# Ten units of the products with B on GpSimd instead of nine, in a four-layer kernel of selective scans

## The chip, the cores and the metric

The kernel runs on one core of one Trainium2 chip. The metric is the device time of one execution in microseconds (us). Engine names follow the profile: PE is TensorE, DVE is VectorE, ACT is ScalarE, POOL is GpSimd, SP is SyncE, which only issues DMAs here.

## The reference

Eight images of 48 x 48 positions with 96 channels pass through four layers, each `x = x + layer(group_norm(x))`. Layers 0 and 3 (l0, l3) are selective scans over four directions of the image (rows and columns, both ways), layer 1 is an upsampling with a two-layer network between, layer 2 (l2) is again four selective scans, but over single rows and columns of 48 positions. The scan at the heart of three of the four layers is

```python
def step(h, inp):
    u, dl, Bv, Cv = inp
    dA = jnp.exp(dl[..., None] * A)
    h = h * dA + (dl * u)[..., None] * Bv[:, :, None, :]
    y = jnp.einsum('bkdn,bkn->bkd', h, Cv)
    return (h, y)
```

for 4 directions, 192 channels and 16 states: per position a product of `dl * u` with B, the recurrence, and a product with C that is summed over the states.

## The kernel before, in words

Each of the three scan layers runs `scans` (L188), which walks through blocks. A block is one image, one direction and 10 of its 48 rows (480 positions, or 8 rows and 384 positions for the last of five): 8 x 4 x 5 = 160 blocks a layer. In l0 and l3 the scan runs on across the rows (a block has 4 columns more for the carried state, so tiles are 481, 484 or 962 wide); in l2 it starts anew at each row.

A block is worked on in four turns, called q0 to q3 here, and each turn in two slots, so slots 0 to 7. A slot holds three units: 3 tiles of 128 partitions (32 channels by 4 states). A turn therefore has six units, and its scans take them in three pairs. The order is written out by hand in the loop at L386 to L418. In turn t:

- DVE: `scan(t, 0)`, `make_dbu(at + 2)`, `scan(t, 1)`, `make_dbu(at + 3)`, `scan(t, 2)`. The scan (L300) is one instruction for two units. `make_dbu` (L268) multiplies `dl * u` by B for the two slots of the next turn, so slots 6 and 7 are made in q2, slots 4 and 5 in q1, slots 2 and 3 in q0.
- POOL: `make_hc(t-1, 1)` (L306, the product with C of a whole slot, in place), then its own part of `make_dbu` for the next turn's two slots, then `begin` (a small copy or zero, L277 or L280), then `make_hc(t, 0)`.
- ACT: `make_da` (L292, the exponential for two units, into one of two PSUM buffers), `copy_b` (L249), and side steps.
- PE: `reduce` (L326, L328), which sums the products with C over the states into `ps_y`, behind the `make_hc` of the turn before, and side steps.

Which units of a slot POOL makes is the table that the change edits: `ON_POOL_SS` for l0 and l3, `ON_POOL_L2` for l2 (L43, L44). The value is the number of the slot's units, its last ones, that POOL makes; DVE makes the others. DVE reads B from a PSUM copy (`ps_b`, one buffer) that ACT writes in `copy_b`; POOL reads B from SBUF. Where a slot is all POOL's, no copy is made:

```python
if on_pool.get(slot) == 3:
    return
if slot == NG // 2 and t - 1 in bps:
    bps[t] = bps[t - 1]
    return
```

so slot 4 takes slot 3's copy over where there was one (in l2).

`aside` (L370) runs, once a slot, the steps that prepare the blocks to come (`stage1`), the end of the outputs (`done`), and a side generator (the convolution of the next image and the normalization of the last one in l0 and l3). Some of these change ACT's function and need a table load before and another before the next exponential. In l0 and l3 it is the softplus (L678) in slot 6, that is in q3, and in part of the blocks the SiLU of the next image's convolution (L538, L540). In l2 it is the SiLU of u (L799) in slot 6, in q3; the softplus (L827) in slot 0, in q0; and the SiLU of the gate, zb (L842), in slot 2, in q1. In l2, PE runs `project` (L864) in slot 2 and the two convolutions (L792) in slots 3 and 4; `done` multiplies `ps_y` by zb on DVE (L855), once in q0 and once in q2; L870 or L872 add the projection in slot 3.

DMAs are all issued on SP: `store_dd` (L446) writes `dl` and `dl * u` to DRAM, `load_dd` (L221) and `load_bc` (L233) bring them back, broadcast over partitions, into three buffers and seven buffers.

Of the kernel before, what the change touches and what calls it, by code (L numbers as in the profile page):

```python
# [39 lines left out]
FAR = 1e30  # L40
CH = 96

ON_POOL_SS = {2: 1, 3: 3, 5: 1, 6: 1, 7: 3}  # L43
ON_POOL_L2 = {3: 2, 5: 3, 6: 1, 7: 3}  # L44


DIRS_SS = [(False, False), (True, False), (False, True), (True, True)]
# [50 lines left out]
def vss_stack_kernel(ctx: ExitStack, tc: tile.TileContext, i: dict, out: bass.AP):  # L98
# [372 lines left out]
    def ss2d(l, xin, xout, b0=0):  # L471
# [41 lines left out]
        def conv(b, blks, behind=lambda step: step()):  # L513
            if blks[0] == BLKS[0]:
                us[b] = big.tile([DH, 2, L], F32, tag="big", name="u")
                zs[b] = zdr.tile([DH, 2, L], F32, tag="z", name="zd")
            for r0, nr in blks:
                n = nr * SEG
                for half in range(2):
                    pu = side_psum()  # L520
                    for slot in range(7):
                        for tap in ((0,), (1, 2), (3,), (4, 5), (6,), (7, 8), ())[slot]:
                            dy, dx = tap // 3, tap % 3
                            at = (2 * tap + half) * DH
                            nc.tensor.matmul(pu[:, :n], lhsT=flat[:, at:at + P],  # L525
                                             rhs=xpad[:, r0 + dy:r0 + dy + nr, dx:dx + W],
                                             start=(tap == 0), stop=(tap == 8))
                        if slot == 6:
                            got = {}

                            def gate():
                                got["z"] = ps("s1", 1)
                                nc.tensor.matmul(got["z"][:DH, :n], lhsT=w[f"{l}_in"][:, (2 + half) * DH:(3 + half) * DH],
                                                 rhs=xpad[:C, 1 + r0:1 + r0 + nr, 1:1 + W], start=True, stop=True)
                            behind(gate)
                        yield
                    s = slice(r0 * W, r0 * W + n)
                    nc.scalar.activation(us[b][:, half, s], pu[:DH, :n], AF.Silu, bias=w[f"{l}_cb"][:, half:half + 1])  # L538
                    z = zp.tile([DH, BMAX], F32, tag="z", name="z")
                    nc.scalar.activation(z[:, :n], got["z"][:DH, :n], AF.Silu)  # L540
                    yield
                    nc.sync.dma_start(zs[b][:, half, s], z[:, :n])
# [164 lines left out]
        for _ in conv(0, BLKS[:1]):  # L707
            pass
        scans(dirs, (0, 1, 3, 2), False, ON_POOL_SS, a, pools, ps, stage1, opening, done, side, tail, conv(0, BLKS[1:3]))
        for _ in post(nb - 1, BLKS[:1]):  # L710
# [4 lines left out]
    def lines(xin, xout):  # L715
# [172 lines left out]
        dirs = DIRS_L2  # L888
        scans(dirs, range(NK), True, ON_POOL_L2, a, pools, ps, stage1, opening, done, side, tail)
        stack.close()  # L890
# [288 lines left out]
```

## Time and profile before

| | us |
|---|---|
| median of 3 runs (18397.58 to 18422.25) | 18410.51 |
| the profiled execution | 18410.93 |
| its span in the trace | 18409.2 |
| scans of l0 in the trace, from 107 to 5561 | 5454 |
| scans of l2, from 6978 to 12808 | 5830 |
| scans of l3, from 12924 to 18381 | 5457 |

The 1.7 us between the execution and its span lie outside the first and last instruction. What is left between the three stretches is layer 1 (5561 to 6978) and short preparations. In the profile, a group's row gives the line, engine, operation, written and read tiles, shape and count, then the busy time, the mean duration in ns, and the idle time before it with what ended it.

### The profile page before, as it was taken

Reading aid. Unit: us, or ns where it says so; the run is one execution under the profiler, and the core shown is the slowest. Engines: PE = TensorE matmul, PEld = TensorE weight load, DVE = VectorE, ACT = ScalarE, POOL = GpSimd, SP = SyncE. Lnnn points to the kernel's source line nnn. Section 1 sums busy time; section 2 is a strip of 40 time slices with the busy share of each in tenths; the row PEclk is TensorE's granted clock in tenths of the full one; section 3 lists DMA queues with packets and bytes.
Section 4 is the critical chain, followed back from the end, with each engine's and each line's share of the span. In section 5 each row is a group of like instructions: output and inputs, shape, how many; then the busy total and the mean of one; then the engine's idle time right before and its main releaser. Section 6 shows DMA issues by size and latency. Waiting matters only on the chain.

```text
span 18409.2 us, 167554 instructions
## 1 busy us (share of the span) xinstructions
PE 14747.1 (80%) x53500; PEld 4297.8 (23%) x53500; DVE 16140.7 (88%) x10329; ACT 13666.8 (74%) x20348; POOL 15136.4 (82%) x7999
## 2 busy tenths in 40 slices
PE   7777777777777897888988988988777777777777
PEld 1211211211214562222222222222121221221221
DVE  7999999999992228999999999997899999999998
ACT  6877887887772227888788888886788778778776
POOL 7999999999990007888888888887899999999998
PEclk7877877777767787888888888888778778777776
DMA  4544545544443324444444444443454455455454
GB/s 143 175 171 171 172 172 172 174 174 167 172 168 52 50 43 148 158 150 152 156 149 156 150 155 156 148 155 125 164 178 171 169 173 173 170 175 173 166 174 144
DMA packets 768448, 2836.47 MB, mean 154 GB/s; under 512 B 235724, under 2 KB 298668, under 8 KB 640926
## 3 DMA queue, kind: packets, MB, share of 16 engines
q1 hardware_dynamic: 767558, 2825.75, 45.4%
q8 instruction: 418, 6.85, 0.2%
q14 instruction: 472, 3.87, 0.1%
HBM read 2377.32 MB, written 448.17 MB: 153 GB/s over the span
## 4 chain that ended last, share of the span: by engine, by line
POOL 27%; PE 20%; DVE 16%; issue 14%; ACT 14%; DMA 8%; SPq 1%; POOLq 0%; ACTq 0%; DVEq 0%
POOL dbu L306 18%; DVE dbu L300 10%; POOL dbu L268 6%; PE ps_s L792 5%; ACT ps_da L292 5%; DVE dbu L268 4%; DMA dd<-dds 3%; POOL dds L460 3%; PE ps_y L326 3%; ACT L292 2%; DMA dd<-dd 2%; PE ps_h L998 2%; PE ps_y L1011 2%; PE ps_s L864 1%; ACT L827 1%
## 5 line engine op out<-in xcount | busy, mean ns | idle before, releaser
L300 DVE TENSOR_TENSOR_SCAN dbu<-ps_da,dbu 128x968 f32<-128x968 f32 (+3 forms) x5760 | 11820.3, 2075 | 559.7 <-ACT ps_da L292 447.5
L306 POOL TENSOR_TENSOR dbu<-dbu,bc 128x1440 f32<-128x1440 f32 (+1 forms) x3840 | 10061.9, 2633 | 1615.3 <-DVE dbu L300 1540.9
L292 ACT ACTIVATE ps_da<-dd,w_l_a 128x484 f32<-128x484 f32 (+3 forms) x11520 | 7433.6, 649 | 2878.2 <-DVE dbu L300 2651.5
L326 PE MATMUL ps_y<-dbu,w_red 128*32 128x480 f32 (+1 forms) x23040 | 4838.4, 735 | 1955.6 <-POOL dbu L306 1935.4
L328 PE MATMUL ps_y<-dbu,w_red 128*32 128x480 f32 (+1 forms) x7680 | 4797.9, 735 | 0.0
L268 DVE TENSOR_TENSOR dbu<-dd,ps_b 128x962 f32<-128x962 f32 (+5 forms) x2880 | 3833.4, 1331 | 264.9 <-ACT ps_b L249 150.6
L268 POOL TENSOR_TENSOR dbu<-dd,bc 128x481 f32<-128x481 f32 (+5 forms) x2240 | 3910.5, 1760 | 22.6 <-DMA dd<-dd 19.5
L326 PEld LDWEIGHTS ps_y<-dbu,w_red 128*32 128x32 f32 x23040 | 748.5, 124 | 5975.6 <-POOL dbu L306 4242.9
L792 PE MATMUL ps_s<-xpad,w_l_cw 128*128 128x480 f32 (+1 forms) x2560 | 1758.5, 839 | 0.0
L249 ACT COPY ps_b<-bc 128x482 f32<-128x482 f32 (+3 forms) x2720 | 1450.5, 533 | 233.4 <-DVE dbu L268 191.4
L525 PE MATMUL ps_side<-xpad,w_l_cw 128*128 128x480 f32 (+1 forms) x2880 | 1526.5, 657 | 18.9 <-ACT u L538 14.2
L292 ACT ACT_TABLE_LOAD x986 | 1265.0, 1283 | 17.6
L734 POOL MEMSET xpad<- 128x2760 f32 x2 | 4.7, 2404 | 1333.9 <-DVE x L978 1333.9
L322 PE MATMUL ps_y<-ysum,w_ident 96*96 96x480 f32 (+1 forms) x960 | 762.9, 885 | 315.9 <-ACT ysum L701 315.3
L650 PE MATMUL ps_s<-bcl,dtw 6*96 6x480 f32 (+1 forms) x1280 | 871.7, 770 | 103.7 <-ACT dds L654 93.2
L660 PE MATMUL ps_s<-u,w_l_xp 96*38 96x480 f32 (+1 forms) x1280 | 832.3, 781 | 20.3 <-ACT z L540 20.3
L460 POOL TENSOR_TENSOR dds<-dds,u 96x960 f32<-96x960 f32 (+1 forms) x320 | 706.8, 2209 | 156.3 <-ACT dds L678 156.3
L525 PEld LDWEIGHTS ps_side<-xpad,w_l_cw 128*128 128x128 f32 x2880 | 559.8, 217 | 1032.4 <-issue 905.2
L792 PEld LDWEIGHTS ps_s<-xpad,w_l_cw 128*128 128x128 f32 x2560 | 521.2, 208 | 1084.6 <-issue 977.2
L328 PEld LDWEIGHTS ps_y<-dbu,w_red 128*32 128x32 f32 x7680 | 687.5, 124 | 0.0
L833 PE MATMUL ps_s<-xpad,w_l_inz 96*96 96x480 f32 (+1 forms) x640 | 506.3, 925 | 86.4 <-ACT dds L827 70.5
L654 ACT ACTIVATE dds<-ps_s,w_l_dtb 96x480 f32<-96x480 f32 (+1 forms) x640 | 404.7, 632 | 212.5 <-PE ps_s L650 94.7
(147 smaller groups left out, 11759.8 us busy)
## 6 DMA issues: line engine op xcount, KB each, us to landing
dd<-dd SPq DMA_DIRECT2D x512, 1452.0 KB
bc<-bcd SPq DMA_DIRECT2D x1536, 480.0 KB
dd<-dd SPq DMA_DIRECT2D x256, 1440.0 KB
dd<-dds SPq DMA_DIRECT2D x512, 363.0 KB
dd<-dd SPq DMA_DIRECT2D x128, 1164.0 KB
bc<-bcd SPq DMA_DIRECT2D x384, 384.0 KB
dd<-dds SPq DMA_DIRECT2D x256, 360.0 KB
dd<-dd SPq DMA_DIRECT2D x64, 1152.0 KB
```

The source lines that it names most:

```text
L249: nc.scalar.copy(bps[t][:, :bcs[t][0].shape[1]], bcs[t][0])
L268: engine.tensor_mul(o, du, by.unsqueeze(1).to_broadcast([P, hi - lo, by.shape[1]]))
L292: nc.scalar.activation(da[:, at:at + b.m], b.got[half][:, u % 3, 0, :], AF.Exp, scale=a[:, b.k, ci:ci + 1])
L300: nc.vector.tensor_tensor_scan(db, da, db, 0.0, ALU.mult, ALU.add)
L306: nc.gpsimd.tensor_mul(h, h, bcs.pop(2 * t + sub)[1].unsqueeze(1).to_broadcast([P, 3, n]))
L326: nc.tensor.matmul(y[32 * g:32 * g + 32, :n], lhsT=wc["red"][:, :32], rhs=hc[:, g, b.at], start=False, stop=(slot == 3))
L328: nc.tensor.matmul(y[DH:, :n], lhsT=wc["red"][:, 32:], rhs=hc[:, 2, b.at], start=(slot == 0), stop=(slot == 3))
L460: nc.gpsimd.tensor_mul(du, dt, u)
L525: nc.tensor.matmul(pu[:, :n], lhsT=flat[:, at:at + P], rhs=xpad[:, r0 + dy:r0 + dy + nr, dx:dx + W], start=(tap == 0), stop=(tap == 8))
L650: nc.tensor.matmul(got["p"][:DH, :n], lhsT=dtw[2 * NS:, b.k, half, :], rhs=b.bcl[2 * NS:, :n], start=True, stop=True)
L660: nc.tensor.matmul(got["p"][:NBC, :n], lhsT=w[f"{l}_xp"][:, b.k, half, :], rhs=u[:, half], start=(half == 0), stop=(half == 1))
L792: nc.tensor.matmul(got["u", half][:, :n], lhsT=flat[:, at:at + P], rhs=shifted(off), start=(tap == 0), stop=(tap == 3))
```

## The change

In l0 and l3, slot 6 has two of its three units on POOL instead of one: ten of a block's 24 units instead of nine. In l2, slot 5 has two instead of three and slot 6 three instead of one: again ten instead of nine. Slots 6 and 7 are made in q2, slot 5 in q1. With that, in l2, `copy_b` makes a copy of B for slot 5, which it did not, and none for slot 6; in l0 and l3 the copies stay as they were.

```diff
-ON_POOL_SS = {2: 1, 3: 3, 5: 1, 6: 1, 7: 3}
-ON_POOL_L2 = {3: 2, 5: 3, 6: 1, 7: 3}
+ON_POOL_SS = {2: 1, 3: 3, 5: 1, 6: 2, 7: 3}
+ON_POOL_L2 = {3: 2, 5: 2, 6: 3, 7: 3}
```

## The prediction

> **What bounds the kernel now.** I read, in this order, the page's shares, the window table of the three scan stretches (l0, l2, l3), the groups kept apart by shape, and the timeline of two blocks. The page's first line leaves VectorE (DVE) and GpSimd (POOL) as the two full engines over the whole span:
>
> ```profile
> PE 14747.1 (80%) x53500; PEld 4297.8 (23%) x53500; DVE 16140.7 (88%) x10329; ACT 13666.8 (74%) x20348; POOL 15136.4 (82%) x7999
> ```
>
> In the window table each row is one stretch of 160 blocks; busy us are in the order PE, PEld, DVE, ACT, POOL (l2, l0, l3):
>
> ```profile
> 6978.00:12808.00 5830.00, 5052.19 (x15956) 1331.77 (x15956) 5391.98 (x3447) 4710.87 (x6754) 4904.94 (x2236) 0.84 0.42 152
> 107.00:5561.00 5454.00, 4156.12 (x15207) 1057.38 (x15205) 5217.40 (x3174) 4292.81 (x6488) 5074.34 (x2843) 0.75 0.49 170
> 12924.00:18381.00 5457.00, 4173.44 (x15204) 1063.66 (x15204) 5217.21 (x3174) 4293.40 (x6487) 5074.18 (x2842) 0.75 0.49 170
> ```
>
> Per block (divide by 160): in l0 and l3 34.1 us, DVE 32.6 (96%), POOL 31.7 (93%). In l2 36.4 us, DVE 33.7 (93%), POOL 30.7 (84%), PE 31.6 (87%), ACT 29.4: no engine is full there, so a chain through several of them sets the pace.
>
> The prices, from the groups by shape (busy us, mean ns):
>
> ```profile
> L268 DVE TENSOR_TENSOR dbu<-dd,ps_b 128x962 f32<-128x962 f32 x768 | 868.2, 1130 | 0.0
> L268 DVE TENSOR_TENSOR dbu<-dd,ps_b 128x480 f32<-128x480 f32 x128 | 80.5, 629 | 0.0
> L268 POOL TENSOR_TENSOR dbu<-dd,bc 128x481 f32<-128x481 f32 x768 | 794.6, 1035 | 0.0
> L268 POOL TENSOR_TENSOR dbu<-dd,bc 128x960 f32<-128x960 f32 x128 | 241.2, 1885 | 22.6 <-DMA dd<-dd 19.5 <-issue 2.7 <-DMA bc<-bcd 0.4
> L268 POOL TENSOR_TENSOR dbu<-dd,bc 128x1443 f32<-128x1443 f32 x512 | 1403.6, 2741 | 0.0
> ```
>
> One unit more costs POOL 0.85 us and saves DVE 0.50.
>
> GpSimd in one l0 block, turns q2 and q3 (start, us, instruction, idle before it):
>
> ```profile
> 3056.71 3.74 POOL L268 TENSOR_TENSOR dbu<-dd,bc 128x481 f32<-128x481 f32 x2
> 3060.41 1.54 POOL L592 TENSOR_TENSOR ysum<-ysum,zin 96x768 f32<-96x768 f32 x1
> 3061.91 5.43 POOL L306 TENSOR_TENSOR dbu<-dbu,bc 128x1440 f32<-128x1440 f32 x2
> 3068.25 2.73 POOL L306 TENSOR_TENSOR dbu<-dbu,bc 128x1440 f32<-128x1440 f32 x1 [0.92 <-DVE dbu L300]
> ```
>
> POOL makes slots 6 and 7, multiplies by C behind the scans, and catches up with DVE only in q3: that wait for a scan is its slack. Tabulated over the blocks of l0 and l3, it is 1.44 us in the mean, 1.5 in the median, but zero in over a tenth of them.
>
> In l2, the same for ACT, PE and DVE from q1 to q2, in one block:
>
> ```profile
> 9726.61 1.20 ACT L292 ACTIVATE ps_da<-dd,w_l_a 128x384 f32<-128x384 f32 x2 [0.70 <-DVE dbu L300]
> 9727.83 1.28 ACT L842 ACT_TABLE_LOAD   x1
> 9729.12 1.02 ACT L842 ACTIVATE zb<-ps_s 96x480 f32<-96x480 f32 x2
> 9730.17 1.28 ACT L292 ACT_TABLE_LOAD   x1
> 9731.46 1.20 ACT L292 ACTIVATE ps_da<-dd,w_l_a 128x384 f32<-128x384 f32 x2
> ```
> ```profile
> 9729.74 2.30 PE L864 MATMUL ps_s<-gated,wo 96*96 96x384 f32 x4
> 9731.88 7.67 PE L792 MATMUL ps_s<-xpad,w_l_cw 128*128 128x480 f32 x8
> ```
> ```profile
> 9741.04 0.55 DVE L855 TENSOR_TENSOR gated<-zb,ps_y 96x384 f32<-96x384 f32 x1 [2.30 <-PE ps_y L328]
> ```
>
> The gate's burst (L842 between two table loads) lets PE start L864, then the convolution L792 at the low clock (7.7 us; 3.4 in other blocks), then the reductions, and DVE waits for those in q2. So where PE is slow, the burst in q1 sets the end of q2.
>
> **What the Trainium skill says.** "SBUF — State Buffer", section "Who interferes with whom": a DVE instruction with one SBUF input does not contend with GpSimd. All DVE products and scans here take their other input from PSUM, and the trace agrees: the 962-element product averages 1130 ns while POOL is 93% busy. So more work on POOL should not stretch DVE's instructions. "ScalarE: Activation LUTs", section "What ACT_TABLE_LOAD costs": 1283 ns each plus a drain. The trace shows 1.28 us, and next to no idle behind it; I use the trace's.
>
> **The change, part by part.** Everything else, queues of SP included, keeps its order.
>
> *l0 and l3 (320 blocks): slot 6 from one unit on POOL to two.* DVE's product in q2 goes from 1130 to 629 ns: -0.50. POOL's from 1035 to 1885: +0.85, in q2, behind the two multiplications by C of q1 and ahead of slot 7 and those of q2. B is copied for slot 6 in both kernels. POOL thus falls 0.85 + 0.50 = 1.35 us further behind DVE. Queued behind it: slot 7's product, the C products of q2, PE's reductions for them. Who waits: the first scan of q3, which now needs POOL's part of slot 6 (before, only the second did). From the timeline, slot 6 is ready 7.3 us in the median (5.7 at the 5th percentile) ahead of the second scan; the first comes 1.55 + 2.08 = 3.6 earlier, which leaves 3.7 and 2.1, less 1.35: still positive. Carrying the added lag through each block's own POOL waits, and letting DVE stop wherever the lag exceeds the lead of a product, gives DVE 0.06 us of new stops a block. DVE's dbu with the shorter blocks saves 0.40 (0.93 to 0.53) instead of 0.50: mean -0.48. I add 0.09, an estimate that I chose, for PE's later side work (L598 before L601) and for ACT's L654, which waits for a DMA in a few blocks and would not move with DVE. Sum -0.48 + 0.06 + 0.09 = -0.33; x 320 = -105. Bounds: -0.45 (nothing lost) to -0.2 (twice that loss), -144 to -64.
>
> *l2 (160 blocks): slot 5 from three units to two, slot 6 from one to three.* DVE gains a product in q1 (+0.629) and loses one in q2 (-1.130). POOL: -0.85 in q1, +1.70 in q2, hidden by its 36.4 - 30.7 = 5.7 us of idle a block; slots 6 and 7 lead their scans by 6.8 and 4.1 at the least; slot 6, needed one scan (3.6) sooner and done 1.7 later, keeps 1.5, and q1 hands POOL over 0.85 earlier. On ACT the copy of B (L249, 0.55) moves: slot 6's, after the burst and the first exponentials of q2, goes; slot 5's comes, *ahead* of the gate's burst. With one PSUM buffer for B it waits for DVE's product of slot 4, which ends 0.0 to 0.15 us after ACT's exponentials; with 0.17 for the semaphore and 0.55 for the copy, the burst starts 0.72 to 0.86, say 0.82, later in every block. Queued behind it: both table loads, zb, the exponentials of q2. Who waits: PE's L864 (in 0.63 us a block on zb already), so L792 and the reductions, and the first scan of q2. That scan comes 0.82 later; q2 is then 1.05 shorter on DVE (1.13 less overlap): -0.23, if nobody else is late. Where DVE already waits at L855 for PE, the whole +0.82 stays. I tabulated each block's lead of the reductions over the end of q2's last scan: some 45% have none, the median is 0.9. The larger of the two paths per block averages +0.25: 63 of 154 blocks, those with the slow L792, take +0.82, the other 91 -0.15. x 160 = +40. Bounds: -0.23 (PE never in the way, -37) and +0.82 (always, +131).
>
> **Sum** against the profiled execution, 18410.9 (span 18409.2; it is the median of the runs within 0.5): 18411 - 105 + 40 = 18346, say **18350**, -0.33%. Differences within 0.2% (37 us) a measurement of this kernel hardly tells from none.
>
> **Rivals.** (a) *The gain is mostly eaten*: -0.2 in l0 and l3, +0.25 in l2: -64 + 40, 18387. For: POOL's slack in q3 is zero in over a tenth of the blocks. (b) *Slower: the copy in front of the gate's burst delays all l2 blocks*, because PE, idle longer before L864, keeps the low clock more often: +131, and l0 and l3 give only -64: 18478. It decides for slower once l0 and l3 give less than (131 - 37)/320 = 0.29 a block. Against: most blocks now have the fast L792. (c) *GpSimd becomes the bound in l0 and l3*: 31.7 + 0.85 = 32.6 of 34.1; if 2.0 us of its 2.4 us of waits re-form each block, the block is 34.6, +0.5 x 320 = +160, with +40: 18611. Against: the leads above. (d) *All of it*: -144 and -24: 18243.
>
> **Chances.** Forecast 40%, (a) 25%, (b) 17%, (c) 8%, (d) 10%. Faster by over 0.2%: 0.50; within: 0.25; slower: 0.25. Range 18260 to 18485: it takes in (b), and leaves out (c) and most of (d).
>
> **What would show it.** In l0 and l3: block 33.8 us, DVE's products 0.5 us less a block, POOL's idle in q3 down from 1.4 to some 0.3, no new DVE waits on POOL. In l2: the copy ahead of L842, q1 longer and q2 shorter by about 0.8 and 1.0, more waiting of L855 on L328. I am wrong if DVE's waits for ACT or POOL in l0 and l3 rise by over 0.3 a block, or if l2 moves by more than 0.8 a block either way.

## The result, and the profile after

The changed kernel takes 18481.54 us in the median of 5 runs (18460.64 to 18483.61), the kernel before, on the same chip, 18406.71: a ratio of 1.0039, 95% interval 1.0027 to 1.005. It is slower by 0.39%, where the prediction had it faster by 0.33%. The profiled execution took 18466.15 us, with a span of 18464.4. It is 55 us longer than the profiled execution of before, while the medians differ by 75; the stretches below account for the 55.

The window table of the changed kernel, one row for each stretch of 160 blocks (l2, l0, l3; busy us in the order PE, PEld, DVE, ACT, POOL, then the granted PE clock, the DMA share and GB/s):

```profile
6982.00:12865.00 5883.00, 5073.00 (x15955) 1347.44 (x15956) 5325.22 (x3447) 4722.07 (x6754) 5037.35 (x2236) 0.83 0.42 151
108.00:5558.00 5450.00, 4207.52 (x15201) 1064.61 (x15202) 5159.80 (x3174) 4294.02 (x6486) 5205.47 (x2843) 0.74 0.49 170
12982.00:18436.00 5454.00, 4204.23 (x15206) 1066.45 (x15206) 5159.77 (x3174) 4294.13 (x6487) 5205.63 (x2843) 0.74 0.49 170
```

Against the table of before: l2 grows from 5830 to 5883, by 53 us, or 0.33 a block (predicted: 40 and 0.25). l0 and l3 shrink from 5454 and 5457 to 5450 and 5454, together by 7 us (predicted: 105). GpSimd has 0.82 us more work a block there ((5205.5 - 5074.3) / 160) and DVE 0.36 less, and the stretch is as long as it was. That DVE's busy time falls by less than the 0.48 of its products has mainly one reason: small instructions of the next image's normalization (L171 to L173, L183), in 14 blocks of a layer, take 49.2 us in all instead of 31.9, or 0.11 us a block more (the last section shows why). What else DVE saved it now spends waiting.

The groups by shape have the prices that the prediction used (busy us, mean ns):

```profile
L268 DVE TENSOR_TENSOR dbu<-dd,ps_b 128x481 f32<-128x481 f32 x256 | 160.9, 629 | 0.0
L268 POOL TENSOR_TENSOR dbu<-dd,bc 128x962 f32<-128x962 f32 x256 | 484.5, 1893 | 0.0
```

GpSimd in the block of l0 that the prediction showed (start, us, instruction, idle before it):

```profile
3050.10 4.59 POOL L268 TENSOR_TENSOR dbu<-dd,bc 128x962 f32<-128x962 f32 x2
3054.65 1.54 POOL L592 TENSOR_TENSOR ysum<-ysum,zin 96x768 f32<-96x768 f32 x1
3056.15 8.25 POOL L306 TENSOR_TENSOR dbu<-dbu,bc 128x1440 f32<-128x1440 f32 x3
```

The two products take 4.59 instead of 3.74, and the 0.92 us that GpSimd waited for a scan is gone: three multiplications by C run without a stop.

Who waits in l3, DVE and ACT (us in all, times, longest). Before:

```profile
DVE dbu L300 <- ACT ps_da L292: 106.3, 133, 3.4
DVE xi L601 <- PE ps_side L598: 42.0, 17, 4.7
DVE dbu L300 <- issue: 37.7, 34, 2.5
DVE dbu L300 <- POOL dbu L306: 12.8, 8, 1.8
...
ACT dds L654 <- PE ps_s L650: 44.0, 45, 3.3
ACT ysum L701 <- PE ps_y L328: 7.3, 15, 1.1
```

After:

```profile
DVE dbu L300 <- ACT ps_da L292: 115.2, 140, 3.5
DVE dbu L300 <- issue: 60.4, 49, 3.2
DVE xi L601 <- PE ps_side L598: 46.6, 17, 4.7
DVE dbu L300 <- POOL dbu L306: 4.4, 3, 1.9
...
ACT dds L654 <- PE ps_s L650: 64.5, 51, 3.4
ACT ysum L701 <- PE ps_y L328: 18.5, 29, 1.5
```

DVE's scans hardly wait for GpSimd. They wait more for ACT's exponentials and for things the profile doesn't name ("issue"), and ACT in turn waits more for PE: its second L654 of a block for the matmul L650, its copy L701 for the last reduction L328. All waits of DVE in l3 that are longer than 0.15 us, added up, grow from 239 to 294 us, 0.34 a block: "issue" by 23, GpSimd by 12, PE by 11, ACT by 8.

### The profile page after: what moved, and what is told of

Read it like the earlier page. It is cut to its first block, busy times and chain, and to the rows that moved or that the text cites. A ratio compares the mean times of both kernels' runs of the same rounds, so it can differ in the third digit from the quotient of the medians.

```text
span 18464.4 us, 167640 instructions
## 1 busy us (share of the span) xinstructions
PE 14864.2 (81%) x53500; PEld 4328.0 (23%) x53500; DVE 15958.9 (86%) x10329; ACT 13681.7 (74%) x20348; POOL 15531.9 (84%) x7999
## 5 line engine op out<-in xcount | busy, mean ns | idle before, releaser
L306 POOL TENSOR_TENSOR dbu<-dbu,bc 128x1440 f32<-128x1440 f32 (+1 forms) x3840 | 10064.7, 2635 | 1292.6 <-DVE dbu L300 1229.5
L326 PE MATMUL ps_y<-dbu,w_red 128*32 128x480 f32 (+1 forms) x23040 | 4898.6, 743 | 1926.2 <-POOL dbu L306 1887.0
L328 PE MATMUL ps_y<-dbu,w_red 128*32 128x480 f32 (+1 forms) x7680 | 4858.5, 743 | 0.0
L268 POOL TENSOR_TENSOR dbu<-dd,bc 128x481 f32<-128x481 f32 (+7 forms) x2240 | 4306.8, 1938 | 19.7 <-DMA dd<-dd 19.3
L268 DVE TENSOR_TENSOR dbu<-dd,ps_b 128x962 f32<-128x962 f32 (+5 forms) x2880 | 3599.8, 1250 | 277.4 <-DMA dd<-dd 92.0
L792 PE MATMUL ps_s<-xpad,w_l_cw 128*128 128x480 f32 (+1 forms) x2560 | 1767.8, 843 | 1.4 <-ACT zb L842 1.4
L525 PE MATMUL ps_side<-xpad,w_l_cw 128*128 128x480 f32 (+1 forms) x2880 | 1542.5, 663 | 23.4 <-ACT u L538 18.4
L292 ACT ACT_TABLE_LOAD x986 | 1265.0, 1283 | 17.4
L650 PE MATMUL ps_s<-bcl,dtw 6*96 6x480 f32 (+1 forms) x1280 | 870.1, 768 | 107.1 <-ACT dds L654 95.9
L660 PE MATMUL ps_s<-u,w_l_xp 96*38 96x480 f32 (+1 forms) x1280 | 877.6, 820 | 18.3 <-ACT z L540 18.3
L525 PEld LDWEIGHTS ps_side<-xpad,w_l_cw 128*128 128x128 f32 x2880 | 568.2, 220 | 1056.9 <-issue 913.2
L792 PEld LDWEIGHTS ps_s<-xpad,w_l_cw 128*128 128x128 f32 x2560 | 531.8, 213 | 1097.0 <-issue 1011.6
L328 PEld LDWEIGHTS ps_y<-dbu,w_red 128*32 128x32 f32 x7680 | 692.5, 125 | 0.0
L654 ACT ACTIVATE dds<-ps_s,w_l_dtb 96x480 f32<-96x480 f32 (+1 forms) x640 | 405.6, 634 | 264.1 <-PE ps_s L650 136.9
```

The source lines that it names most:

```text
L268: engine.tensor_mul(o, du, by.unsqueeze(1).to_broadcast([P, hi - lo, by.shape[1]]))
L292: nc.scalar.activation(da[:, at:at + b.m], b.got[half][:, u % 3, 0, :], AF.Exp, scale=a[:, b.k, ci:ci + 1])
L306: nc.gpsimd.tensor_mul(h, h, bcs.pop(2 * t + sub)[1].unsqueeze(1).to_broadcast([P, 3, n]))
L326: nc.tensor.matmul(y[32 * g:32 * g + 32, :n], lhsT=wc["red"][:, :32], rhs=hc[:, g, b.at], start=False, stop=(slot == 3))
L328: nc.tensor.matmul(y[DH:, :n], lhsT=wc["red"][:, 32:], rhs=hc[:, 2, b.at], start=(slot == 0), stop=(slot == 3))
L525: nc.tensor.matmul(pu[:, :n], lhsT=flat[:, at:at + P], rhs=xpad[:, r0 + dy:r0 + dy + nr, dx:dx + W], start=(tap == 0), stop=(tap == 8))
```

## The experiments

All are timed against the kernel before on the same chip. "e1" and so on are short names for the labels. Each table of units is given as its changed lines.

**Which half of the change costs?** Each half alone:

```diff
 e1:
-ON_POOL_SS = {2: 1, 3: 3, 5: 1, 6: 1, 7: 3}
+ON_POOL_SS = {2: 1, 3: 3, 5: 1, 6: 2, 7: 3}
 e2:
-ON_POOL_L2 = {3: 2, 5: 3, 6: 1, 7: 3}
+ON_POOL_L2 = {3: 2, 5: 2, 6: 3, 7: 3}
```

Expected of e1: 

> Only l0 and l3 get the tenth unit (slot 6: 2), l2 as before. Theory A (ACT's chain from the first scan of q2 over the biased step times, PE's L650 and the softplus burst to the next block's first exponentials covers what DVE saves): 0 to -20 us against before. Theory B (GpSimd's lag makes DVE wait for its products): 0 to -20 as well, but then with DVE waits on POOL in q3. If the changed kernel's loss came from l0 and l3 after all: +50 or more.

Measured: 18414.03, ratio 1.0006 (0.9998 to 1.0014): no change.

Expected of e2: 

> Only l2 gets its new table (slot 5: 2, slot 6: 3). If the two halves add up: +50 to +80 us against before, all of it in the l2 stretch. If the halves interact: less than +30 or more than +100.

Measured: 18459.63, ratio 1.0034 (1.0021 to 1.0047). Within the noise the whole loss is l2's; l0 and l3 give nothing either way.

**Is it the copy ahead of the gate's burst (l2)?** e3 is the kernel before, and only makes that copy of B:

```diff
-if on_pool.get(slot) == 3:
+if on_pool.get(slot) == 3 and not (restart and slot == 5):
```

Expected: 

> The kernel before, and in l2 one more copy of B, for slot 5, which nobody reads: it sits ahead of the gate's burst as in the changed kernel, while DVE's and GpSimd's shares stay as before. Theory A (the copy delays the burst by 0.82 us and with it PE and the first scan of q2): +100 to +131 us, 0.6 to 0.82 a block. Rival (DVE's added product in q1 is what costs): under +30.

Measured: 18501.9, ratio 1.0054 (1.0041 to 1.0067), and l2 grows from 5830 to 5919 us, 0.56 a block. The copy alone costs more than the whole change of l2, which gives part of it back through DVE's shorter q2. Where the copy stands is seen in the changed kernel, on ACT, PE and DVE, in one block:

```profile
9794.38 0.56 ACT L249 COPY ps_b<-bc 128x480 f32<-128x480 f32 x1 [0.18 <-DVE dbu L268]
...
9794.97 1.28 ACT L842 ACT_TABLE_LOAD   x1
...
9796.88 1.53 PE L864 MATMUL ps_s<-gated,wo 96*96 96x384 f32 x4 [0.51 <-ACT zb L842]
...
9798.25 7.67 PE L792 MATMUL ps_s<-xpad,w_l_cw 128*128 128x480 f32 x8
...
9807.73 0.65 DVE L855 TENSOR_TENSOR gated<-zb,ps_y 96x480 f32<-96x480 f32 x1 [1.48 <-PE ps_y L328]
```

The copy waits 0.18 for DVE's product of slot 4, takes 0.56, and only then the burst begins; PE waits for zb, runs the slow convolution, and DVE waits 1.48 us at the end of q2. DVE's wait at L855 (us in all, times) before, after and in e3:

```profile
  PE ps_y L328: 86.2, 84
```

```profile
  PE ps_y L328: 161.7, 105
```

```profile
  PE ps_y L328: 86.2, 87
```

In e3 this wait is what it was, so the end of q2 is not where the copy alone costs. It costs in q1, where DVE adds the projection L864 (L870, L872) and so waits for zb too. Those who waited for L864, before and in e3:

```profile
  DVE x L872: 41.8, 48
  DVE x L870: 25.0, 29
```

```profile
  DVE x L872: 96.3, 109
  DVE x L870: 64.3, 40
```

Tabulated from the traces, e3's q1 is 0.75 longer than before (8.84 to 9.59 in the mean), its q2 as long, and its q3 0.19 shorter, since DVE waits less there for the load of `dd` (43.7 us before, 15.4 in e3, over l2). In the changed kernel these two waits for L864 come to 101.5 us, as DVE's added product of q1 fills part of the time, and the wait at L855 nearly doubles once DVE has one product less in q2.

The slow convolution is not a matter of the clock, as the prediction had it. A matmul of L792 takes 1122 ns in the median for the blocks of the two directions that run over columns (935 for their short blocks), and 564 (484) for those over rows, in every image before the change. In the block that the prediction showed, PE's reductions ahead of the slow L792 and right behind it:

```profile
9726.95 0.86 PE L326 MATMUL ps_y<-dbu,w_red 128*32 128x384 f32 x3
...
9739.48 0.52 PE L326 MATMUL ps_y<-dbu,w_red 128*32 128x384 f32 x3
```

Those behind run at the fast one of their two rates. For the split by blocks that changes nothing: the blocks whose PE runs the slow L792 are half of all, and they grow by 0.69 us in the changed kernel (36.71 to 37.40), the others by -0.03 (36.22 to 36.19); predicted were 0.82 and -0.15.

e4 takes the unit on GpSimd where no copy is needed ahead of the burst, and leaves slot 5 alone (`ON_POOL_L2 = {3: 2, 5: 3, 6: 2, 7: 3}`). Expected: 

> In l2 the tenth unit goes to slot 6 alone (1 to 2), slot 5 stays wholly on GpSimd, so that no copy moves. Theory A: -20 to -50 us, from the blocks in which PE is not in the way at the end of q2 (some 91 of 154, at 0.3 to 0.5). Rival (GpSimd or PE bounds q2 in all blocks): 0 or slower.

Measured: 18397.3, ratio 0.9999 (0.999 to 1.0007). The loss is gone, but what DVE saves (0.46 us a block in the trace) is no gain here either: DVE waits more for PE at L855 at the end of q2 (counted within the stretch of l2, 80.8 us before and 113.8 in e4) and, in q3, for the load of `dd` (43.7 and 70.4), together 0.37 a block.

**Where does DVE's saving go in l0 and l3?** My first theory (A) was ACT's chain with the softplus burst at its end; the rival (B) that GpSimd's later products stop DVE. e5 and e6 have no softplus burst, with nine and ten units (an exponential stands in its place, so the computation is changed); e7 and e8 put the tenth unit into q1 and q0 instead:

```diff
 e5, e6:
-nc.scalar.activation(both, both, AF.Softplus)
+nc.scalar.activation(both, both, AF.Exp)
 e6: ON_POOL_SS = {2: 1, 3: 3, 5: 1, 6: 2, 7: 3}
 e7: ON_POOL_SS = {2: 1, 3: 3, 5: 2, 6: 1, 7: 3}
 e8: ON_POOL_SS = {2: 2, 3: 3, 5: 1, 6: 1, 7: 3}
```

Expected of e5: 

> The kernel before, but the softplus of the step sizes in l0 and l3 is an exponential (that part of the computation is changed), so that ACT needs no table load there: ACT's burst in q3 falls from 3.6 to 1.0 us. Theory A: ACT's chain in q3 goes, the blocks of l0 and l3 become 0.3 to 0.9 us shorter: -100 to -290 us. Theory B: -100 at most.

Measured: 18387.44, ratio 0.9991 (0.9982 to 0.9999).

Expected of e6: 

> The same with an exponential in place of the softplus of l0 and l3, and slot 6 of l0 and l3 with two units on GpSimd. Theory A: with ACT's burst out of the way, what DVE saves counts: 0.2 to 0.48 a block below the kernel with the exponential and nine units, -65 to -155 us. Theory B (GpSimd's lag): no gain on it, or a loss.

Measured: 18391.26, ratio 0.9994 (0.9985 to 1.0002).

The burst costs ACT two table loads of 1.28 us a block (the Trainium skill, "ScalarE: Activation LUTs", section "What ACT_TABLE_LOAD costs", has 1283 ns, which the trace confirms); without them the execution is 19 us shorter by the medians (2 to 33 by the interval), some 0.06 a block, and the tenth unit still brings nothing. The burst alone is not what covers DVE's saving.

Expected of e7: 

> In l0 and l3 the tenth unit goes to slot 5 (1 to 2), which DVE and GpSimd make in q1, where ACT is not on the path; l2 as before. Theory A: DVE's 0.48 us are saved ahead of the first scan of q2, where ACT's chain starts: 0.3 to 0.48 a block, -95 to -155 us. Theory B: GpSimd carries the same load as with slot 6: 0 or slower.

Measured: 18445.71, ratio 1.0023 (1.0014 to 1.0032).

Expected of e8: 

> In l0 and l3 the tenth unit goes to slot 2 (1 to 2), made in q0, where GpSimd lags most; l2 as before. Theory A: DVE's 0.48 us are saved in q0, but slot 3's product now leads its scan by 1.4 us less and that lead is 1.4 at the least, 3.4 in the median: -60 to -140 us. Theory B: slower, by DVE waits on POOL in q1.

Measured: 18476.9, ratio 1.0039 (1.0026 to 1.0051). Both cost time, although DVE saves as much. So it seems that something behind GpSimd's work of q0 and q1 is on the path, more than what stands behind its work of q2.

**Is it GpSimd's time at all?** f1 and f2 take one of the three units of slot 3's product with C away, just ahead of slot 6 on GpSimd (it is left out of the computation); f1 has ten units, f2 nine:

```diff
+w = 2 if not restart and q == 1 and sub == 1 else 3
-nc.gpsimd.tensor_mul(h, h, ...to_broadcast([P, 3, n]))
+nc.gpsimd.tensor_mul(h[:, :w], h[:, :w], ...to_broadcast([P, w, n]))
```

Expected of f1: 

> Slot 6 of l0 and l3 with two units on GpSimd (l2 as before), and GpSimd's product with C of slot 3, which stands just ahead of it, on two of the slot's three units: one unit of this product is left out of the computation. It takes some 0.95 us a block off GpSimd, at the place where the change puts 0.85. Theory C (what DVE saves is lost because GpSimd's added work makes its products with C later, behind which PE keeps its own side matmuls and so ACT and DVE their side steps): with GpSimd no later, DVE's saving stays, -0.33 to -0.48 a block in l0 and l3, 18250 to 18300 us. Rival D (GpSimd has no part in it; another chain of fixed length, on ACT or in the DMAs, sets the pace of a block): no gain, 18390 to 18415, the same as with the full product.

Measured: 18305.22, ratio 0.9945 (0.9932 to 0.9957).

Expected of f2: 

> The same relief of GpSimd (one of the three units of slot 3's product with C left out, in l0 and l3), with nine units as before. It gives what the relief is worth alone. Theory C as far as nine units already feel GpSimd: up to -0.15 a block, 18355 to 18405. Rival D: no change, 18390 to 18415. Were it worth as much as with ten units (-100 us or more), GpSimd would be the bound of both kernels.

Measured: 18399.92, ratio 0.9997 (0.9989 to 1.0005).

This is the clearest pair of the study. The relief is worth nothing with nine units and 0.55% with ten: -106 us, -0.33 a block, the saving that the prediction had counted on. So with nine units the time of this product of GpSimd is not on the path that ends last, and with ten it is, in a block of almost the same length. Whether the path runs from the product to PE, or through the products that stand behind it on GpSimd, the pair doesn't tell.

f3 and f4 have no table loads in l0 and l3 at all (softplus as in e5, and the two SiLU of L538 and L540 as Identity), with nine and ten units. Expected of f3: 

> Nine units, and in l0 and l3 no burst of table loads at all: the softplus of the step sizes is an exponential, and the two SiLU of the convolution and of its gate are plain additions of the bias; these parts of the computation are changed. The base for the next run. Theory C: table loads are not the cover, within 50 us of the run with the softplus alone replaced, 18340 to 18400. Rival E (ACT's bursts, those of the convolution too, are what ends last): -0.3 a block and more, below 18300.

Measured: 18328.28, ratio 0.9956 (0.9944 to 0.9969).

Expected of f4: 

> The same without any burst of table loads in l0 and l3, and slot 6 with two units on GpSimd. Against the run before it: theory C: no gain (-20 to +30 us), since GpSimd's lag is unchanged. Rival E: the full saving of DVE, -0.33 to -0.48 a block, -100 to -150 us.

Measured: 18381.74, ratio 0.9984 (0.9977 to 0.999). The convolution's bursts cost some 64 us (0.9956 against 0.9991 in e5), but they don't hide the saving: without them the tenth unit costs 53 us, more than I had put down for any theory.

**Is it a lag that builds up over blocks?** Then ten units in only some blocks would keep part of the saving. Four choices of blocks (counted in each image, 0 to 19):

```diff
+more = not restart and slot == 6 and t // NG % 20 in TEN_IN
-cut = 3 - on_pool.get(slot, 0)
+cut = 3 - on_pool.get(slot, 0) - more
```

g1, every second block. Expected: 

> l2 as before; in l0 and l3 slot 6 has two units on GpSimd in every second block and one in the others. Theory C (the saving is lost where GpSimd has no idle left, and a block's lag is shed in GpSimd's idle time of the next): half the saving is offered, 0.24 a block, and most of it is kept: -30 to -70 us, 18335 to 18380. Rival G (any added product on GpSimd in q2 is paid in full in its own block): 18395 to 18415, as with ten units in all blocks.

Measured: 18405.6, ratio 1.0 (0.9992 to 1.0008).

g2, blocks 8 to 19. Expected: 

> l2 as before; in l0 and l3 slot 6 has two units on GpSimd in blocks 8 to 19 of each image, those without steps of the normalization, one in blocks 0 to 7. Rival F (the loss sits in the normalization's steps, whose product L592 is GpSimd's too, and whose PE and DVE steps wait for one another): 12 of 20 blocks keep the saving, 192 x -0.4: about -75 us, 18330. Theory C (in these blocks GpSimd's idle is as short): -10 to -40, 18365 to 18395.

Measured: 18409.19, ratio 1.0002 (0.9993 to 1.001).

g3, blocks 0 to 7. Expected: 

> The complement: two units in blocks 0 to 7 of each image, one in blocks 8 to 19. Rival F: all of the loss and none of the saving, 128 x 0 to +0.2: 18405 to 18435. Theory C: near no change as well, 18390 to 18420; below 18370 would say that the loss sits in the convolution's blocks.

Measured: 18398.77, ratio 0.9997 (0.9989 to 1.0005).

g4, the nine blocks with the most idle GpSimd. Expected: 

> Two units only in the nine blocks of an image (1, 2, 3, 5, 7, 9, 10, 15, 16) in which GpSimd was idle for some 1.75 us or more in the trace of the kernel before. Theory C: the saving is kept there, 144 blocks x -0.3 to -0.48: -45 to -70 us, 18335 to 18365, faster than nine units everywhere and than ten. Rival D (GpSimd's lag is not the cause): no change, 18390 to 18415.

Measured: 18405.05, ratio 1.0 (0.9992 to 1.0008). All four are no change. The gains that theory C, the lag, had for g1 and g4 didn't come, so idle time of GpSimd in a block doesn't keep the saving. That all of it is lost within its own block is not shown: in the trace of g1 the ten-unit blocks are shorter than the same blocks before (by 0.06 in l0 and 0.19 in l3), and the nine-unit blocks between them longer (by 0.15 and 0.20).

**Is it a chain of fixed length from the first scan of q2?** The relief of f1 also shortened such a chain, seen here before the change in one block of l0, on all engines:

```profile
3321.81 2.73 POOL L306 TENSOR_TENSOR dbu<-dbu,bc 128x1440 f32<-128x1440 f32 x1
...
3322.10 2.17 DVE L300 TENSOR_TENSOR_SCAN dbu<-ps_da,dbu 128x968 f32<-128x968 f32 x1 [0.53 <-ACT ps_da L292]
...
3324.59 1.02 PE L326 MATMUL ps_y<-dbu,w_red 128*32 128x480 f32 x3 [1.68 <-POOL dbu L306]
...
3326.35 2.65 PE L525 MATMUL ps_side<-xpad,w_l_cw 128*128 128x480 f32 x4
...
3328.92 1.04 PE L650 MATMUL ps_s<-bcl,dtw 6*96 6x480 f32 x2
...
3330.00 0.66 ACT L654 ACTIVATE dds<-ps_s,w_l_dtb 96x480 f32<-96x480 f32 x1
3330.56 2.64 ACT L292 ACTIVATE ps_da<-dd,w_l_a 128x484 f32<-128x484 f32 x4
...
3333.62 1.28 ACT L678 ACT_TABLE_LOAD   x1
...
3335.94 1.28 ACT L292 ACT_TABLE_LOAD   x1
```

When the last scan of q1 is done, the first of q2 starts on DVE and the product with C of slot 3 on GpSimd, 2.73 us. Behind it PE reduces, does a side step and L650, whose result ACT needs for its second L654; behind that, in order, stand the exponentials of q3, the softplus and the exponentials of the next block. Nothing in this row depends on DVE's product of slot 6. h1 and h2 were to cut L650 out of the chain, with ten and nine units, by PE's order alone:

```diff
-if t > 0:
+if t > 0 and (restart or q != 2):
     reduce(t - 1, 1)
 aside(at)
+if not restart and q == 2:
+    reduce(t - 1, 1)
```

Expected of h1: 

> Ten units in l0 and l3, l2 as before, nothing left out: on PE alone, in q2 of l0 and l3, the side steps of slot 4 (L650 with its step sizes for the second half among them) are issued ahead of the reductions for slot 3 instead of behind them. So L650 no longer waits for GpSimd's product with C of slot 3, which starts with the first scan of q2; GpSimd's work and order stay those of ten units. Theory A' (a chain of fixed length from the first scan of q2 over GpSimd's product with C, PE's reductions, L650, ACT's L654 and the softplus to the exponentials of the next block keeps the block as long as it was; the relief helped because it shortened this chain): -0.25 to -0.45 a block, 18260 to 18325. Theory C' (the relief helped because it took GpSimd's lag away from the products that come after): no gain, 18390 to 18420.

Measured: 18490.26, ratio 1.0048 (1.0035 to 1.0062).

Expected of h2: 

> The same swap on PE with nine units: what it is worth alone. Theory A': with nine units the chain is not what ends last, or not by much: -30 to +10 us, 18370 to 18415. Theory C': no change, 18390 to 18415; a gain of 80 us or more would say that PE's order was the bound of the kernel before, whatever the units.

Measured: 18500.58, ratio 1.0052 (1.0039 to 1.0065).

Neither theory had this. The waits of h2 in l3 (its lines behind L408 are two higher: L656 is L654, L703 is L701) say why:

```profile
DVE dbu L300 <- ACT ps_da L292: 148.1, 156, 4.5
...
ACT ysum L703 <- PE ps_y L328: 127.4, 111, 5.0
ACT dds L656 <- DMA dd<-dds: 40.8, 26, 3.2
```

The wait of L654 for L650 is gone, as meant (44 us before). But the reductions now stand behind the side steps, and L650 among these waits for ACT's first L654; so the copy L701, which is ahead of the second L654 on ACT, waits 127 us for them instead of 7. I had exchanged one entrance to the chain for a later one. So the runs did not free the chain; they lengthened it, with GpSimd's work untouched, and the block grew, with nine units and with ten. In f1 the same waits are shorter than before (its lines behind L306 are one higher, so L655 is L654):

```profile
DVE dbu L300 <- ACT ps_da L292: 83.1, 107, 3.4
...
ACT dds L655 <- PE ps_s L651: 25.0, 29, 3.3
ACT ysum L702 <- PE ps_y L329: 9.9, 18, 1.5
```

Tabulated from the traces, the mean over the blocks of l3 (blocks 2 to 156), us from the start of the first scan of q2:

| | last matmul of L650 starts | second L654 starts | second scan of q3 | next block's first scan | block |
|---|---|---|---|---|---|
| before (9 units) | 6.55 | 8.11 | 11.15 | 17.41 | 33.96 |
| f2 (9, relief) | 5.87 | 7.98 | 11.17 | 17.37 | 33.92 |
| h2 (9, swap) | 5.47 | 8.62 | 11.33 | 17.69 | 34.24 |
| after (10) | 6.53 | 7.94 | 10.93 | 17.36 | 33.94 |
| e1 (10) | 6.52 | 7.90 | 10.91 | 17.36 | 33.96 |
| f1 (10, relief) | 5.91 | 7.66 | 10.76 | 17.04 | 33.60 |
| h1 (10, swap) | 5.44 | 8.41 | 11.05 | 17.50 | 34.13 |
| e7 (10, in q1) | 7.22 | 8.52 | 11.31 | 17.78 | 34.09 |
| e5 (9, no softplus burst) | 6.98 | 8.49 | 11.39 | 17.34 | 33.93 |
| e6 (10, no softplus burst) | 7.03 | 8.38 | 11.31 | 17.34 | 33.94 |

From before to after, the scan behind DVE's shorter product starts 0.48 earlier, but L650 only 0.02, the second L654 0.17, the second scan of q3 0.22, and the next block 0.05. Where the chain is shorter (f1), the second L654 moves 0.45 and the block 0.36; where it starts later (e7) or is longer (h1, h2), the block is longer. DVE's idle time, tabulated over the same blocks, shows where the saving goes:

| idle time of DVE, us a block | before | f2 | after | f1 | e5 | e6 |
|---|---|---|---|---|---|---|
| between the first two scans of q3 | 0.16 | 0.16 | 0.27 | 0.11 | 0.27 | 0.47 |
| ahead of the next block's first scan | 0.47 | 0.41 | 0.62 | 0.49 | 0.18 | 0.26 |
| all | 1.39 | 1.32 | 1.73 | 1.48 | 1.40 | 1.77 |

Of the 0.34 that the change adds, 0.26 stands in these two places, which lie behind the second L654. In e5, without the burst, the next block's first scan waits for ACT no more, but L650 and the second L654 lie some 0.4 later than before (why, the runs don't show), and the tenth unit (e6) moves the second L654 by only 0.11. There the second scan of q3 gains 0.08 and the block nothing: the row holds the block at that scan already, ahead of where the burst stood.

## Why the prediction was wrong

**The prices of the moved work were right.** DVE's product fell from 1130 to 629 ns and GpSimd's rose from 1035 to 1893. DVE's products and scans did not stretch with more work on GpSimd: the remaining 962-element products (slots 2 and 5, l0 and l3) average 1129 ns against 1130. For them the sentence taken from the Trainium skill, "SBUF — State Buffer", section "Who interferes with whom", held. But I went from them to all of DVE's instructions, and the small ones of the normalization, with both inputs in SBUF, did stretch: 0.11 us a block for which the sum had no term. The blocks that hold them became 0.37 us longer (37.32 to 37.70), the others 0.06 shorter.

**The step that failed is the sum for l0 and l3, -0.48 + 0.06 + 0.09 = -0.33, in its last term.** The 0.06 for new stops of DVE on GpSimd was about right: DVE's waits for GpSimd are 24.5 us in l3 before (L306 and L280) and some 36 after, 0.07 more a block. The 0.09 that I chose for PE's later side work and for L654 stood for a whole chain, and it measured about 0.40: all of the saving but 0.02. Some 0.11 of it are the stretched instructions, and 0.27 new waits of DVE beyond those on GpSimd. I had counted every reader of the instruction that moves, and not asked which second path leads from the same starting point to the end of the block. DVE was 96% busy, so I took its time for the time of the block. A path over GpSimd, PE and ACT was as long as DVE's to within 0.05 a block: f2 shows that this path is not what bounds the nine-unit kernel, and f1 that it, or another with the same first step, bounds the ten-unit one. (A slip in the sum besides: the bound called "nothing lost" is -0.48, or -154 us, not -0.45.)

**The sign test I had written down was the wrong one.** I looked for waits of DVE on POOL or ACT to rise by over 0.3 a block. In l3, the scans' wait for ACT rose by 9 us in 160 blocks, 0.06, and that of all of DVE for GpSimd by 0.07; most of the rest is "issue" (0.14) and PE (0.07). No single row would have given it away; the sum of DVE's idle time does. GpSimd's wait for a scan in q3 (l0, tabulated) fell from 1.37 to 0.58 a block, not to 0.3.

**l2 was right, in mechanism and nearly in size**: +0.25 a block predicted, +0.33 measured. The burst starts 0.77 after the exponentials in the block shown (0.18 + 0.56 and the gap to the load), 0.82 was predicted; q1 is longer by 0.82 (8.83 to 9.65, means over the blocks tabulated from the traces) and q2 shorter by 0.56 (8.04 to 7.48). The prediction's two paths, 63 of 154 blocks with no gain in q2 and the others with all of it, come to 0.25 - 0.82 = -0.57 there in the mean; the 1.0 under what would show it was the gain without PE in the way. DVE's wait at L855 rose by 0.47 a block. The copy alone (e3) costs 0.56. Wrong were the reason for the slow L792, which goes by direction and not by the clock, and what holds the first scan of q2 back: more than the exponentials, DVE's own wait at L870 and L872 for PE's projection.

**Rival (b)** named l2's copy as what could turn the sign, at 18478, with 0.29 a block in l0 and l3 as the point from which it decides. Its two sizes were off, l2 at 53 us instead of 131 and l0 and l3 at 7 instead of 64, and these offset each other. Its reason for l2, the low clock, fits L864 (566 ns before in the median, 643 after) but not L792, which is slow in the same blocks before and after. That is a likeness of totals, not a confirmation. (c), GpSimd as the bound, is not what the runs show: GpSimd still waits in most blocks, and giving it idle blocks (g4) brings nothing.

**What is shown and what stays open.** Shown: without GpSimd's 0.9 us in front of slot 6 the saving stays (f1 against f2); taking away the softplus burst or the convolution's bursts, or choosing the blocks, does not bring it back (e5, e6, f4, g1 to g4); lengthening the row L328, L701, L654 lengthens the block with nine and with ten units (h1, h2). Argued from the table, not shown by a run of its own: that in the changed kernel it is this row, and not GpSimd's products behind slot 6, that holds the block; f1 helped both, and h1 freed neither. In f4, where ACT has no bursts, the tenth unit costs 0.17 a block, and GpSimd's first product with C of q2 starts 1.0 us later than in f3 (in l3, 8.03 against 7.05 after the first scan of q2), so there GpSimd itself may be the bound. Of the new idle time of DVE, "issue" has the largest part, and what it stands for is open. A swap that moves L650 alone, without L525 and the other side steps, was not tried.

No version here beats the kernel before with the whole computation; the nearest, e4 and g3, are within its noise. What f1 suggests is to have 0.9 us of GpSimd's work ahead of slot 6 in another place; this was not tried with the whole computation.

## What to carry to other kernels

An engine that is 96% busy is a candidate for the bound, not the bound. Before counting its saved time as gained, find the last instruction that its path shares with others. From there, follow every other path to the end of the loop's round, over engines that are less busy too, and compare the lengths. The cheap test is a pair: shorten the suspected second path in the kernel before and in the changed one; a path that hides the saving is worth nothing in the first and the whole saving in the second. And where work moves onto an engine that is read through a copy, look at where the copy lands on the engine that makes it: a copy of 0.56 us ahead of a burst of table loads cost 0.56 a block, as much as the moved work could bring.

## What the runs showed of the hardware that I had not expected

PE's matmuls come at two rates. In the block shown, each group of three reductions behind a wait of 1.68 us takes 1.02 us and the convolution's matmuls follow at the same pace (2.65 us for four); in the same block of the changed kernel, behind a wait of 1.13 us, such a group takes 0.60:

```profile
3322.51 0.60 PE L326 MATMUL ps_y<-dbu,w_red 128*32 128x480 f32 x3 [1.13 <-POOL dbu L306]
...
3323.46 1.88 PE L525 MATMUL ps_side<-xpad,w_l_cw 128*128 128x480 f32 x4
```

The same four of the convolution take 1.88. The granted clock goes with it: 0.61 over 3324.5 to 3328.9 in the kernel before, 1.00 over 3322.4 to 3327 in the changed one. In this pair the longer wait on PE was followed by slower work, and L650, which stands behind it on PE and ahead of the second L654, started 6.82 us after the first scan of q2 before and 5.15 after. In l2 the L864 that waits longer for zb has a median of 643 ns after against 566 before. But it is no rule that a longer wait is followed by the slow rate, as the kernel before shows 18 us later:

```profile
3342.60 0.60 PE L326 MATMUL ps_y<-dbu,w_red 128*32 128x480 f32 x3 [2.59 <-POOL dbu L306]
```

The Trainium skill, "TensorE: Matmul & The Clock Gate", section "Part 1: The HAM clock gate (the "warmup" mystery)", describes such a pair of rates, one half the other, set by how busy PE was in a window of some 3.4 us. The ratio agrees in part (1.02 to 0.60, and 2.65 to 1.88 where the rate changes on the way). Over all of l0 and l3 the granted clock is 0.74 to 0.75. Which of the waits bring the slow rate was not measured.

A matmul can be slow at the fast rate too: L792 reads its image over columns in half of the blocks, and takes 1122 ns there instead of 564, while the reductions behind it run fast. The order of reading is the difference that the program shows; no run changed it alone.

DVE instructions of one element a partition can take as long as a GpSimd product. L171 to L173 and L183 have both inputs in SBUF. In one block of l3, DVE and GpSimd before, and the same block after:

```profile
13866.74 1.31 DVE L171 TENSOR_TENSOR dev<-mv,gm 96x1 f32<-96x1 f32 x1
13864.31 3.73 POOL L268 TENSOR_TENSOR dbu<-dd,bc 128x481 f32<-128x481 f32 x2
```

```profile
13926.33 2.66 DVE L171 TENSOR_TENSOR dev<-mv,gm 96x1 f32<-96x1 f32 x1
13924.39 4.59 POOL L268 TENSOR_TENSOR dbu<-dd,bc 128x962 f32<-128x962 f32 x2
```

Both times L171 ends within 0.02 us of the GpSimd product that was running (13868.05 and 13868.04, 13928.99 and 13928.98), and L172, which follows it, ends with the GpSimd instruction after that. Where no GpSimd product runs on, such an instruction takes 0.15 us (L173). With ten units GpSimd's product ends later, and DVE with it.
